# Feed-forward of a decoder layer: banks, the addition of z, and two folded constants

## The chip, the cores and the metric

The kernel runs on one core of a Trainium2 chip. The metric is device time in microseconds of one execution, from the chip. Before the change the median of three runs is 3090.13 us (3086.34 to 3092.24). A core has engines that work side by side, each with its own queue of instructions: TensorE (PE in the profile, with its weight loads as PEld), VectorE (DVE), ScalarE (ACT), GpSimd (POOL) and SyncE (SP), which here issues DMAs. SBUF is the working memory of 128 partitions; PSUM has eight banks, each holding 128x512 fp32 values, and matmuls write there.

## What is computed

One decoder layer in fp32 over 2048 tokens of width 512: self-attention over a gathered cache, cross-attention, and a feed-forward part with a low-rank correction; each is added to its input and then normalised. The feed-forward part, where the change lies:

```python
z = jnp.einsum('bsd,od->bso', x, W) + b
u = jnp.einsum('bsd,edr->ebsr', x, A)
m = jnp.einsum('ebsr,ero,e->bso', u, B, p_scores)
norm_z = jnp.linalg.norm(z, axis=-1, keepdims=True)
norm_m = jnp.linalg.norm(m, axis=-1, keepdims=True)
gamma = jnp.minimum(C_CLAMP * norm_z / (norm_m + EPS), 1.0)
return z + gamma * m
...
x = _layernorm(x + ffn(x))
```

C_CLAMP is 0.5, EPS is 1e-6, the small term of the layer norm is 1e-5.

## The kernel before

Tokens stand in four blocks of 512 (tb = 0 to 3), each of four row tiles of 128 tokens (i = 0 to 3). `acc[tb]` holds the running sum with tokens on partitions, `xT[tb]` the same with features on partitions. Self-attention comes first (to about 1900 us), then keys and values of the cross-attention, then 32 cross-attention units (8 groups of heads by 4 blocks), and last the feed-forward part of each block.

The loop over units (variable n) is software-pipelined: in step n stand the queries and scores of unit n and the attention (`attend`) and output projection (`project`, seven matmul steps on three PSUM banks x, y, z) of unit n−1. When the last group of a block is projected, the block is normalised (`layernorm_parts`, lines L149 to L157) and a step later transposed (`transpose_block`, L129 and L131; two of its four copies are VectorE's and two ScalarE's). The feed-forward calls lie at the end: block 0 at the end of step 31; then, in the closing step 32, the transposes of block 2, `attend(31)`, the feed-forward of block 1, the projection of unit 31; after it blocks 2, then the transposes of block 3, then block 3.

TensorE and GpSimd work in program order from step 31 on: their order is written out by hand. VectorE's and ScalarE's orders are chosen there by a scheduler when the program is built; on the chip every engine then takes its queue strictly in order.

`feed_forward(tb)` per block: pu (L1172, the low-rank u, four chunks of features, two matmuls each), uT (L1176, VectorE scales pu out of PSUM). Then for each row tile: pz (L1186, four chunks) and pm (L1185, one chunk, needs uT), pm standing between the second and third chunk of pz; sqm (L1191) and sqz (L1195), ScalarE's squares summed into `nrm`; z = pz + bias by VectorE (L1193); acc + z by GpSimd (L1196); nrm's root by ScalarE (L1197); four small VectorE instructions that make gam (L1199 to L1202); acc += gam times pm (L1203, VectorE); the layer norm of the tile: statistics (L167, L169), rstd = variance + small term (L171, VectorE), its root (L172, ScalarE), its reciprocal (L173, VectorE), the scaling of acc (L174, VectorE); and the store (L1206).

PSUM's eight banks in this part: four of tag ps, handed out in turn (queries, projections, transposes, pu, pz, pm); two of tag sc (scores of a unit); po0 and po1 (`pp`, the first half of `attend`'s result, `pox`). `bank` gives a tile of tag ps.

Of the kernel before, what the change touches and what calls it, by code (L numbers as in the profile page):

```python
# [9 lines left out]
F32 = mybir.dt.float32  # L10
I32 = mybir.dt.int32
AF = mybir.ActivationFunctionType
ALU = mybir.AluOpType
# [3 lines left out]
P = 128  # L17
DIM = 512
# [4 lines left out]
TB = 512  # L23
NTB = NT // TB
TPB = TB // P
NC = DIM // P
# [19 lines left out]
LN_EPS = 1e-5  # L46
NORM_EPS = 1e-6
CLAMP = 0.5
# [4 lines left out]
def decoder_layer(  # L53
# [30 lines left out]
    nc = tc.nc  # L84

    const = ctx.enter_context(tc.tile_pool(name="const", bufs=1))
# [5 lines left out]

    ident = const.tile([P, P], F32, name="ident")
    make_identity(nc, ident)
    bk = const.tile([P, NKV], F32, name="bk")
    bv = const.tile([P, NKV], F32, name="bv")

# [21 lines left out]
    def bank(shape, name, tag=None):  # L119
        if tag in special:  # L120
            v = special[tag]
            return v.rearrange("p (a b) -> p a b", a=shape[1])
        return psum[-1].tile(shape, F32, tag=tag or "ps", name=name)
# [17 lines left out]
    def layernorm_parts(tb, name):  # L141
        a = acc[tb]
        rstd = small.tile([P, TPB], F32, tag="rstd", name=f"rstd_{name}_{tb}")
        mv = small.tile([P, TPB, 2], F32, tag="mv", name=f"mv_{name}_{tb}")

        def stats():
            for j in range(TPB):
                st = small.tile([P, 6], F32, tag="st", name=f"st_{name}_{tb}_{j}")
                nc.vector.bn_stats(st, a[:, j, :])  # L149
                nc.vector.bn_aggr(mv[:, j, :], st)  # L150
            nc.vector.tensor_scalar_add(rstd, mv[:, :, 1], LN_EPS)
            nc.scalar.activation(rstd, rstd, AF.Sqrt)

        def scale():
            nc.vector.reciprocal(rstd, rstd)
            for j in range(TPB):
                nc.vector.tensor_scalar(  # L157
                    a[:, j, :], a[:, j, :], mv[:, j, 0:1], rstd[:, j : j + 1],
                    ALU.subtract, ALU.mult,
                )  # L160

        return stats, scale

    def layernorm_tile(tb, j, name):
        a = acc[tb][:, j, :]
        st = small.tile([P, 6], F32, tag="st", name=f"st_{name}_{tb}_{j}")
        nc.vector.bn_stats(st, a)  # L167
        mv = small.tile([P, 2], F32, tag="mv1", name=f"mv_{name}_{tb}_{j}")
        nc.vector.bn_aggr(mv, st)  # L169
        rstd = small.tile([P, 1], F32, tag="rstd1", name=f"rstd_{name}_{tb}_{j}")  # L170
        nc.vector.tensor_scalar_add(rstd, mv[:, 1:2], LN_EPS)  # L171
        nc.scalar.activation(rstd, rstd, AF.Sqrt)  # L172
        nc.vector.reciprocal(rstd, rstd)  # L173
        nc.vector.tensor_scalar(a, a, mv[:, 0:1], rstd, ALU.subtract, ALU.mult)  # L174

# [288 lines left out]
    with ExitStack() as ph:  # L464
# [3 lines left out]
        sc = ph.enter_context(tc.tile_pool(name="sc", bufs=2, space=PSUM))  # L468
# [309 lines left out]
        c = first.c  # L778
        first.step(1)
        first.step(2)  # L780
        z = first.mul("z", 5, True)
# [156 lines left out]
    with ExitStack() as ph:  # L938
# [23 lines left out]
        with ExitStack() as st:  # L962
# [16 lines left out]
            for k, (gp, tb) in enumerate(pairs):  # L979
                if gp == 1:  # L980
                    stats, scale = layernorm_parts(tb, "a")
# [29 lines left out]
        sc = ph.enter_context(tc.tile_pool(name="xsc", bufs=2, space=PSUM))  # L1011
        pp = ph.enter_context(tc.tile_pool(name="xpo", bufs=1, space=PSUM))
# [154 lines left out]

        def feed_forward(tb):
            wf, af, bm = ffn_w
            pu = bank([P, TB], f"pu{tb}")  # L1170
            for c in range(NC):
                nc.tensor.matmul(  # L1172
                    pu, af[:, c, :], xT[tb][:, c, :], start=(c == 0), stop=(c == NC - 1)
                )
            uT = sb.tile([P, TB], F32, tag="uT", name=f"uT{tb}")
            nc.vector.tensor_scalar(uT, pu, pe, None, ALU.mult)  # L1176
            for i in range(TPB):
                u = f"{tb}_{i}"
                cols = slice(i * P, (i + 1) * P)
                a = acc[tb][:, i, :]  # L1180
                pz = bank([P, DIM], f"pz{u}")
                pm = bank([P, DIM], f"pm{u}")
                for c in range(NC):
                    if c == 2:
                        nc.tensor.matmul(pm, uT[:, cols], bm, start=True, stop=True)  # L1185
                    nc.tensor.matmul(  # L1186
                        pz, xT[tb][:, c, cols], wf[:, c, :], start=(c == 0), stop=(c == NC - 1)
                    )
                nrm = small.tile([P, 2], F32, tag="nrm", name=f"nrm{u}")
                sqm = sb.tile([P, DIM], F32, tag="en", name=f"sqm{u}", bufs=3)  # L1190
                nc.scalar.activation(sqm, pm, AF.Square, accum_out=nrm[:, 1:2])  # L1191
                z = sb.tile([P, DIM], F32, tag="en", name=f"z{u}", bufs=3)
                nc.vector.tensor_tensor(z, pz, bz, ALU.add)  # L1193
                sqz = sb.tile([P, DIM], F32, tag="en", name=f"sqz{u}", bufs=3)
                nc.scalar.activation(sqz, z, AF.Square, accum_out=nrm[:, 0:1])  # L1195
                nc.gpsimd.tensor_tensor(a, a, z, ALU.add)  # L1196
                nc.scalar.activation(nrm, nrm, AF.Sqrt)  # L1197
                gam = small.tile([P, 1], F32, tag="gam", name=f"gam{u}")
                nc.vector.tensor_scalar_add(gam, nrm[:, 1:2], NORM_EPS)  # L1199
                nc.vector.reciprocal(gam, gam)  # L1200
                nc.vector.tensor_tensor(gam, gam, nrm[:, 0:1], ALU.mult)
                nc.vector.tensor_scalar(gam, gam, CLAMP, 1.0, ALU.mult, ALU.min)  # L1202
                nc.vector.scalar_tensor_tensor(a, pm, gam, a, ALU.mult, ALU.add)  # L1203
                layernorm_tile(tb, i, "f")
                r0 = tb * TB + i * P
                nc.sync.dma_start(out=out[r0 : r0 + P, :], in_=a)  # L1206
# [42 lines left out]
        for n in range(N + 1):  # L1249
# [6 lines left out]
            if n < N:  # L1256
                g, tb = units[n]
# [28 lines left out]
            if n == N:  # L1286
                feed_forward(1)
# [6 lines left out]
            if n < N and g == 0:  # L1294
                for j in range(TPB):
                    a = acc[tb][:, j, :]
# [20 lines left out]
            if n == N - 1:  # L1317
                feed_forward(0)
        scales.pop(0)()
        feed_forward(2)  # L1320
        while later:
            later.pop(0)()
# [50 lines left out]
```

## Time and profile before

| | |
|---|---|
| median of three runs | 3090.13 us |
| the profiled execution's own time | 3088.83 us |
| its span, first to last instruction | 3085.9 us |
| busy: TensorE / VectorE / ScalarE / GpSimd | 3034.2 / 2186.5 / 757.2 / 967.6 us |
| granted TensorE clock, mean over the span | 0.997 |

Where the last 120 us go, by windows of the trace (us in the window, then busy us of each engine with the number of instructions, the granted clock, the DMA share and GB/s):

```profile
2960.00:2980.00 20.00, 20.00 (x67) 12.35 (x66) 15.90 (x37) 4.16 (x10) 1.27 (x1) 1.00 0.12 26
2980.00:3000.00 20.00, 18.35 (x65) 8.83 (x63) 18.54 (x44) 7.43 (x23) 6.04 (x5) 1.00 0.11 41
3000.00:3020.00 20.00, 19.96 (x57) 10.86 (x58) 14.98 (x37) 7.10 (x23) 7.90 (x7) 1.00 0.10 39
3020.00:3040.00 20.00, 19.02 (x63) 11.41 (x62) 14.68 (x38) 2.36 (x8) 1.27 (x1) 1.00 0.07 27
3040.00:3060.00 20.00, 17.10 (x52) 8.25 (x51) 17.71 (x42) 6.22 (x21) 3.81 (x3) 1.00 0.14 53
```

The columns are PE, PEld, DVE, ACT and POOL. A busy TensorE means that a matmul was in its pipeline. In a timeline row stand the start in us from the span's start, the length, the engine, the line, the operation, what it writes and reads, and in brackets how long the engine had been idle before it and what ended that.

### The profile page before, as it was taken

What the parts mean: (1) busy time and instruction counts of PE and PEld (TensorE: products, weight loads), DVE (VectorE), ACT (ScalarE), POOL (GpSimd) and SP (SyncE); (2) the same over time, 40 slices, a digit from 0 to 9 for tenths busy, and PEclk for the clock granted to TensorE, in tenths of its full rate; (3) what the DMA queues carried; (4) which work ended last, traced back from release to release, by engine and by line L of the source; (5) the groups of instructions that cost most, each with busy time, mean ns of one, the idle gap of its engine ahead of it and who ended that gap; (6) DMA issues with size and microseconds to landing.
All of it is one profiled execution on the core that took longest, in us unless ns stands there. A gap on an engine that the chain in (4) does not pass through costs nothing.

```text
span 3085.9 us, 42306 instructions
## 1 busy us (share of the span) xinstructions
PE 3034.2 (98%) x14944; PEld 2320.6 (75%) x14944; DVE 2186.5 (71%) x3957; ACT 757.2 (25%) x1760; POOL 967.6 (31%) x789
## 2 busy tenths in 40 slices
PE   8999999999999999999999999999999999999998
PEld 6777677777777777777777769988888888888764
DVE  6777877877877877877877764436656666666677
ACT  2323232232332232232232221211111111111122
POOL 4221322321321322322322123136444444454421
PEclk9999999999999999999999999999999999999999
DMA  6444444444444444444344343321121121121101
GB/s 210 115 115 119 113 115 122 111 122 114 109 126 115 103 129 113 106 126 115 100 125 112 96 122 138 110 96 52 52 69 49 49 69 49 49 68 49 48 28 41
DMA packets 200913, 298.66 MB, mean 97 GB/s; under 512 B 44160, under 2 KB 94848, under 8 KB 200704
## 3 DMA queue, kind: packets, MB, share of 16 engines
q1 hardware_dynamic: 187328, 282.51, 33.8%
q10 hardware_dynamic: 11328, 9.26, 1.0%
q0 software_dynamic: 2048, 4.20, 0.5%
q8 instruction: 120, 1.97, 0.3%
q14 instruction: 89, 0.73, 0.1%
HBM read 107.05 MB, written 20.97 MB: 41 GB/s over the span
## 4 chain that ended last, share of the span: by engine, by line
PE 91%; DVE 4%; DMA 2%; SPq 2%; ACT 1%; issue 1%; ACTq 0%; DVEq 0%
PE po L661 15%; PE s L615 15%; PE sx L1043 2%; PE pox L1114 2%; PE w_0y L282 1%; PE q_3y L282 1%; PE wx_2y L282 1%; PE wx_1y L282 1%; PE w_3y L282 1%; SPq L653 1%; PE qx_2y L282 1%; PE qx_3y L282 1%; PE qx_0y L282 1%; PE w_1y L282 1%; PE q_2y L282 1%; PE wx_0y L282 1%
## 5 line engine op out<-in xcount | busy, mean ns | idle before, releaser
L623 ACT ACTIVATE p<-s,nmax 128x576 f32<-128x576 f32 x512 | 380.4, 743 | 1207.7 <-DVE nmax L620 1207.6
L615 PE MATMUL s<-kT,qT 128*128 128x288 f32 x2048 | 577.9, 408 | 10.4 <-ACT p L623 9.7
L661 PE MATMUL po<-pT,v 128*128 128x512 f32 (+1 forms) x1280 | 549.2, 602 | 4.1 <-DMA pT<-T 4.1
L615 PEld LDWEIGHTS s<-kT,qT 128*128 128x128 f32 x2048 | 387.5, 190 | 115.0 <-issue 20.1
L620 DVE TENSOR_REDUCE nmax<-s 128x1 f32<-128x576 f32 x512 | 384.4, 751 | 47.6 <-PE s L615 47.1
L641 DVE STREAM_TRANSPOSE T<-p 128x576 f32<-128x576 f32 x512 | 394.5, 770 | 4.4
L661 PEld LDWEIGHTS po<-pT,v 128*128 128x128 f32 (+1 forms) x1280 | 213.7, 189 | 204.1 <-issue 177.0
L633 DVE TENSOR_SCALAR p<-p,den 128x576 f32<-128x576 f32 x512 | 324.2, 633 | 17.9
L632 DVE RECIPROCAL den<-den 128x1 f32<-128x1 f32 x512 | 84.1, 164 | 238.1 <-ACT p L623 238.1
L256 POOL TENSOR_TENSOR so<-oT,oT 128x512 f32<-128x512 f32 x32 | 42.5, 1327 | 648.5 <-ACT oT L684 648.5
L258 POOL TENSOR_TENSOR so<-oT 128x512 f32<-128x512 f32 x32 | 40.7, 1271 | 334.4 <-PE w_1y L282 93.0
L1222 POOL TENSOR_TENSOR txx<-x1T 128x512 f32<-128x512 f32 x31 | 39.5, 1275 | 229.5 <-PE qx_3z L282 93.1
L197 POOL TENSOR_TENSOR tx<-xT 128x512 f32<-128x512 f32 x31 | 39.7, 1280 | 206.6 <-PE q_3z L282 65.4
L623 ACT ACTIVATION_READ_ACCUMULATOR p<-s,nmax 128x1 f32 x512 | 99.7, 195 | 0.0
L256 POOL TENSOR_TENSOR sox<-oTx,oTx 128x512 f32<-128x512 f32 x32 | 40.5, 1267 | 184.1 <-DVE oTx L1134 178.6
L1060 ACT ACTIVATE ex<-ex 128x512 f32<-128x512 f32 x64 | 39.4, 632 | 203.2 <-DVE ex L1059 203.2
L684 ACT COPY oT<-po 128x512 f32<-128x512 f32 x128 | 72.0, 588 | 44.6 <-PE po L661 44.0
L1043 PEld LDWEIGHTS sx<-kvx,qTx 128*64 128x64 f32 x2048 | 62.3, 138 | 10.6 <-issue 10.6
L1132 ACT ACTIVATE oTx<-pox,bv 128x256 f32<-128x256 f32 x128 | 52.1, 472 | 67.6 <-PE pox L1114 67.6
L1043 PE MATMUL sx<-kvx,qTx 128*64 128x64 f32 x2048 | 66.7, 224 | 0.0
L1114 PE MATMUL pox<-pTx,kvx 64*128 64x256 f32 x512 | 64.9, 390 | 1.1 <-DMA pTx<-Tx 1.1
L1134 DVE TENSOR_SCALAR oTx<-pox,bv 128x256 f32<-128x256 f32 x128 | 53.6, 479 | 11.2 <-PE pox L1114 11.2
(445 smaller groups left out, 5778.5 us busy)
## 6 DMA issues: line engine op xcount, KB each, us to landing
pT<-T SPq DMA_DIRECT2D x1020, 80.0 KB, 2.1
pT<-T SPq DMA_DIRECT2D x1016, 64.0 KB, 2.0
xT<-in_xT SPq DMA_DIRECT2D x31, 1024.0 KB, 5.6
kvx<-kv SPq DMA_DIRECT2D x32, 512.0 KB, 3.2
pTx<-Tx SPq DMA_DIRECT2D x256, 64.0 KB, 2.0
kv<-c SPq DMA_DIRECT2D x30, 512.0 KB, 3.3
wo<-in_woT SPq DMA_DIRECT2D x32, 256.0 KB, 2.9
xwq<-in_xwq SPq DMA_DIRECT2D x32, 256.0 KB, 2.6
```

What stands on the lines that cost most here:

```text
L256: nc.gpsimd.tensor_tensor(t[1], a[1, 0], a[1, 1], ALU.add)
L282: nc.tensor.matmul(self.banks[b][:, m, :], self.left[i][:, k, m * P : (m + 1) * P], self.right[i][:, k, :], start=(first and m + k == 0), ...
L615: nc.tensor.matmul(s[:, a, :HALF], qTs[n // REP][:, units[n][2], i * P : (i + 1) * P], kTs[g][:, a * HALF : (a + 1) * HALF], start=True, s ...
L620: nc.vector.tensor_reduce(nmax, s[:, :, :HALF], AX.XY, ALU.max, negate=True)
L623: nc.scalar.activation(p.rearrange("q (a k) -> q a k", a=2), s[:, :, :HALF], AF.Exp, bias=nmax, accum_out=den,)
L632: nc.vector.reciprocal(den, den)
L633: nc.vector.tensor_scalar(p, p, den, None, ALU.mult)
L641: nc.vector.transpose(Ts[n][:, :, i, :], ps_.pop((n, i)).rearrange("q (b k) -> q b k", k=SQ))
L661: nc.tensor.matmul(pos[n].rearrange("d (a q) -> d a q", a=NQD), vs[units[n][0]][rows, v, :], pTs[n // 2][rows, :, chunk, :], skip_group_ch ...
L684: nc.scalar.copy(o[:, i, :].rearrange("d (t a k) -> d a t k", t=TPB, a=NQD), pos.pop(n - 1 + i).rearrange("d (a t k) -> d a t k", a=NQD, t ...
L1043: nc.tensor.matmul(s[b * SEQ : (b + 1) * SEQ, i * REP + h, :], qTs[n][:, h, pr * HF + c0 : pr * HF + c0 + SEQ], kvs[n][:, pr, 0, c0 : c0 + ...
L1114: nc.tensor.matmul(po[pr, b][:, i, :].rearrange("d (h a j) -> d h a j", h=REP, a=2), kvs[n][r, pr, 1, i * HD : (i + 1) * HD], pTs[n][r, :, ...
```

## The change

Four edits, all but the first constant in the feed-forward part:

- A constant tile eps holds the layer norm's small term; ScalarE's root in `layernorm_tile` takes it as its bias, and VectorE's separate addition (L171) is gone. `layernorm_parts`, used for the other norms, is as it was.
- pu takes a bank of tag sc, pm takes po0 or po1 by turns; pz alone is left with the four ps banks. In the first tile of a block pm stands behind all four chunks of pz, in the other three as before.
- acc + z is made by VectorE in place of GpSimd.
- The clamp's 0.5 goes into the square of z as its scale (so `nrm` holds half of z's norm), and the last two of the four small gam instructions become one.

```diff
+    eps = const.tile([P, 1], F32, name="eps")
+    nc.gpsimd.memset(eps, LN_EPS)
...
-        nc.vector.tensor_scalar_add(rstd, mv[:, 1:2], LN_EPS)
-        nc.scalar.activation(rstd, rstd, AF.Sqrt)
+        nc.scalar.activation(rstd, mv[:, 1:2], AF.Sqrt, bias=eps)
...
-            pu = bank([P, TB], f"pu{tb}")
+            pu = sc.tile([P, TB], F32, tag="sc", name=f"pu{tb}")
...
-                pm = bank([P, DIM], f"pm{u}")
+                pm = pp.tile([P, DIM], F32, tag=f"po{i % 2}", name=f"pm{u}")
                 for c in range(NC):
-                    if c == 2:
-                        nc.tensor.matmul(pm, uT[:, cols], bm, start=True, stop=True)
                     nc.tensor.matmul(
                         pz, xT[tb][:, c, cols], wf[:, c, :], start=(c == 0), stop=(c == NC - 1)
                     )
+                    if c == (NC - 1 if i == 0 else 1):
+                        nc.tensor.matmul(pm, uT[:, cols], bm, start=True, stop=True)
...
-                nc.scalar.activation(sqz, z, AF.Square, accum_out=nrm[:, 0:1])
-                nc.gpsimd.tensor_tensor(a, a, z, ALU.add)
+                nc.scalar.activation(sqz, z, AF.Square, scale=CLAMP, accum_out=nrm[:, 0:1])
+                nc.vector.tensor_tensor(a, a, z, ALU.add)
...
-                nc.vector.tensor_tensor(gam, gam, nrm[:, 0:1], ALU.mult)
-                nc.vector.tensor_scalar(gam, gam, CLAMP, 1.0, ALU.mult, ALU.min)
+                nc.vector.tensor_scalar(gam, gam, nrm[:, 0:1], 1.0, ALU.mult, ALU.min)
```

In the program as built after the change the instructions of all engines stand as before up to pu of block 0, eps's memset aside. From there VectorE's queue has, per tile, the reciprocal of tile i directly behind its statistics and ahead of z of tile i+1, then the scaling of acc of tile i, then the addition of z of tile i+1. VectorE's four copies out of pox of unit 31, which stood among the small instructions of block 0's last tile, stand behind that tile. GpSimd's queue ends with the sums of unit 31's attention.

## The prediction

> **What bounds the kernel now.** I read the page first (shares of busy time), then the chain of waits, then the timeline of the last 120 us, where all edits but one lie.
>
> ```profile
> PE 3034.2 (98%) x14944; PEld 2320.6 (75%) x14944; DVE 2186.5 (71%) x3957; ACT 757.2 (25%) x1760; POOL 967.6 (31%) x789
> ...
> PE 91%; DVE 4%; DMA 2%; SPq 2%; ACT 1%; issue 1%; ACTq 0%; DVEq 0%
> ```
>
> TensorE is busy 98% of the span and carries 91% of the chain, so nothing in the attention stages can win or lose from this change: there all engines keep their instructions and their order. The changed part starts at 2967.85 us with pu of block 0 and ends with the kernel at 3085.9. In those 118 us the chain of waits runs mostly through VectorE. One row tile of block 2, from the timeline (start, length, engine, instruction, idle before):
>
> ```profile
> 3046.38 0.68 DVE L1193 TENSOR_TENSOR z<-pz,bz 128x512 f32<-128x512 f32 x1
> ...
> 3046.98 0.15 DVE L173 RECIPROCAL rstd_f<-rstd_f 128x1 f32<-128x1 f32 x1
> 3047.14 1.27 POOL L1196 TENSOR_TENSOR acc<-acc,z 128x512 f32<-128x512 f32 x1 [3.59 <-DVE rstd_f L173]
> 3047.16 0.63 ACT L1195 ACTIVATE sqz<-z 128x512 f32<-128x512 f32 x1 [0.46 <-DVE rstd_f L173]
> 3047.17 1.53 DVE L174 TENSOR_SCALAR acc<-acc,mv_f,rstd_f 128x512 f32<-128x512 f32 x1
> ...
> 3047.91 0.20 ACT L1197 ACTIVATE nrm<-nrm 128x2 f32<-128x2 f32 x1
> ...
> 3048.62 0.14 DVE L1199 TENSOR_SCALAR gam<-nrm 128x1 f32<-128x1 f32 x1
> ...
> 3057.24 0.15 DVE L171 TENSOR_SCALAR rstd_f<-mv_f 128x1 f32<-128x1 f32 x1
> 3057.43 0.20 ACT L172 ACTIVATE rstd_f<-rstd_f 128x1 f32<-128x1 f32 x1 [4.06 <-DVE rstd_f L171]
> ...
> 3057.66 0.16 DVE L173 RECIPROCAL rstd_f<-rstd_f 128x1 f32<-128x1 f32 x1 [0.27 <-ACT rstd_f L172]
> 3057.86 0.55 DVE L174 TENSOR_SCALAR acc<-acc,mv_f,rstd_f 128x512 f32<-128x512 f32 x1
> ```
>
> See that L174 lasts 1.53 us when GpSimd's addition starts just ahead of it and 0.55 when GpSimd is idle. From one L174 to the next (3042.31 to 3047.17) a tile takes 4.86 us on VectorE; TensorE needs ten matmul slots of 0.43 us, 4.29. So VectorE sets the pace by 0.57 us a tile.
>
> TensorE between blocks 0 and 1:
>
> ```profile
> 2990.96 1.09 PE L129 MATMUL x<-ident,acc 128*128 128x128 f32 x8 [1.08 <-DVE z L1193]
> 2991.98 2.35 PE L1114 MATMUL pox<-pTx,kvx 64*128 64x256 f32 x16
> 2994.26 3.70 PE L1172 MATMUL pu<-x1T,af 128*128 128x512 f32 x8
> 2997.79 1.88 PE L1186 MATMUL pz<-wf,x1T 128*128 128x512 f32 x4
> 3000.04 1.10 PE L1185 MATMUL pm<-bm,uT 128*128 128x512 f32 x2 [0.37 <-DVE uT L1176]
> ```
>
> The last unit's attention (pox) runs here without waiting for the block's norms, and pm of block 1 is what waits, for uT.
>
> **What the Trainium skill says.** "SBUF — State Buffer", Who interferes with whom: VectorE's two-port forms, tensor_scalar among them, and GpSimd share a port pair that one holds for its whole instruction while the other is blocked. The trace agrees (1.53 against 0.55). "VectorE: DVE Perf Modes", What auto-detection actually checks: tensor_tensor gets no doubled rate for fp32. The trace agrees: `ex<-ex,denx`, also fp32 in SBUF, 686 ns for 512 elements. "TensorE: Matmul & The Clock Gate", What's actually happening: an idle window of about 3.4 us halves the clock. After 4.05 us of idling at 2907.07 the granted clock is 0.50 here; after 2.06 us (1821.23) eight matmuls took their usual time.
>
> **The change part by part**, on the profiled execution's clock. "gam(b,i)" is the start of the first gam instruction (L1199) of tile i of block b.
>
> *VectorE adds z; small terms.* Per tile, start to start. Before: L174 1.44, gam chain to L1203 0.83, L1203 0.78, statistics 0.73 and 0.22, L171 0.07, z 0.60, reciprocal 0.19: 4.86. After, in the changed order (reciprocal, then z, L174, the addition, gam): the three gam instructions left 0.64 (one of 0.19 gone); L1203 0.78; statistics 0.73; aggregate to reciprocal 0.46, since L171 no longer stands between and VectorE waits for ScalarE's root (0.18 + 0.04 + the 0.24 seen at 3057.43 to 3057.66); reciprocal 0.19; then z to gam. On VectorE that is 0.60 + 0.48 (L174 without GpSimd; four L157 take 1.91) + 0.60 to 0.67 for the addition, taken from the 0.69 of the nearest rows, 1.68 to 1.75; through ScalarE it is what it was, z start to gam 1.78 (3062.91 to 3064.69). The later one counts, 1.77. Sum 4.57 to 4.58, so 0.29 less a tile, not the 0.98 that L174 loses: the addition takes most of it back. Bounds: 4.29 (TensorE's pace, if VectorE is faster than I think) to 4.86 (the 0.27 wait for the root is longer, all gained lost). TensorE's 4.29 stays below.
>
> *pm behind all of pz in a block's first tile.* sqm now starts after pz, and ScalarE does sqm (0.70), sqz (0.75), nrm (0.24) in a row: gam at pm's end + 1.73. In block 0 pm ends at 75.74 (times from here on less 2900), so gam at 77.5, as before (77.50, from a z at 75.78); the addition is hidden in this wait. Where pm waited for uT, the wait is covered by two more pz chunks.
>
> *Banks, block 0 to 1.* gam(0,0) 77.50, three tiles to 91.24. Two copies x1T (0.60 each) fall between the addition and the last gam, as before: L1203 of tile 3 starts at 93.09 and ends 93.84 (before 95.23). But its pm now lies in bank po1, and pox's second matmul writes po1. It waits there, with everything behind it on TensorE's hand-written order: the rest of pox, pu(1), pz(1,0). TensorE is there at 91.2 and idles about 2.7 us. Then pox 1.75, pu 3.44, pz 3.44, pm with its end 1.02, ScalarE 1.73: gam(1,0) at 105.3, before 104.67. So 0.6 is lost where 1.4 was ahead: this wait costs 2.0.
>
> *Block 1 and the last projection.* Three tiles: 0.87 less, gam(1,3) 0.24 early. TensorE ends the block at 116.3, does three projection steps (5.19) to 121.46 and the second x step; before, that step started at 121.27, held by L353. It is now held by TensorE itself, 0.2 later, without the 0.26 wait shown inside it, so the projection ends where it did. Balance 0.
>
> *Block 2.* pu ends at 131.9, pz follows without waiting for uT (134.15), pm ends 136.32, gam(2,0) 138.05 against 138.88: 0.83 ahead. Tiles 0.87: 1.70. *Block 3.* pu starts after the x1T copies, 1.7 ahead; pu to gam is 9.63 for 9.78: 0.15. Tiles 0.87. Tail gam to L174: 2.82 for 3.17: 0.35. **Sum: 1.70 + 0.15 + 0.87 + 0.35 = 3.1 us.**
>
> *Hidden or nil.* The memset of eps (0.1 us) falls into GpSimd's 1.50 us wait before its first gather at 3.40. Square's scale and the root's bias change operands, not lengths (bounds: 0 to 0.02 each, 16 tiles, off the sum). pu in bank sc frees a bank nobody was late for. eps moves later tiles in SBUF by a few bytes; no row of the trace shows a length that hangs on a tile's place (pT<-T and pTx<-Tx, 64 KB each, both land in 2.0 us).
>
> Own execution: 3088.83 − 3.1 = 3085.7. It lies 1.3 below the median of 3090.13; in proportion the forecast is **3087.0**. About 0.2%, 6.2 us, is what a measurement of this kernel can tell from no change, and 3.1 is half of that.
>
> **Rivals.**
> *A, the clock halves* in the 2.7 us idling before pox: priced by 2907.07, where 8 matmuls took 3.54 and 2.80 for 1.73: 2.9 us. All later blocks move: 3089.9. Against: 2.7 is short of the 4.05 that did it.
> *B, faster:* TensorE becomes the bound (4.29 a tile) and the wait at po1 is not felt. From the forecast: block 0's 0.87 and the 2.0, of which block 1 keeps all as TensorE carries it; blocks 2 and 3 another 0.87 each: 3.1 + 0.87 + 2.0 + 1.74 = 7.7, time 3082.4. For: TensorE's 4.29 is near. Against: the po1 wait is in the order, and ScalarE's 1.77 doesn't shrink. A part of it plus the spread of the runs shown (3086.34 to 3092.24) can also carry a true 4 beyond 6.2.
> *C, slower:* VectorE's reciprocal now waits on ScalarE's queue, where sqm of the next tile (0.60 + 0.20) stands ahead of the root, and z, L174, the addition all stand behind that reciprocal. If sqm comes late, 0.80 is added in each of the 12 tiles that have a next one: +9.6 − 3.1, time 3096.6. It decides from the point where pm of tile i+1 ends later than 0.74 before the aggregate of tile i ends. Against: block 0's first tile has pm at 78.3, the aggregate at 79.84, 0.8 us to spare, and more in later ones.
> *D, the change doesn't do it:* L174 stays at 1.5 without GpSimd. Then the addition comes on top, about 0.7 a tile, 3098. The 0.55 above speaks against it.
>
> **Numbers.** Forecast 0.62, A 0.10, B 0.20, C 0.06, D 0.02. A and the forecast are within 0.2%: 0.72; faster 0.20; slower 0.08. Range: the forecast's own bounds 3084 to 3090, widened by the spread of runs and towards B: 3082 to 3092.
>
> **What would show it.** L174 near 0.55 in all 16; no GpSimd addition after the last sums; a tile every 4.6 us; a wait of 2 to 3 us of TensorE for L1203 before pox; the reciprocal idle about 0.3 after the aggregate. Wrong if tiles stay at 4.86 or fall to 4.3, if the clock drops after that wait, or if the first 2967 us change.

## The result and the profile after

| | before | after |
|---|---|---|
| median, 22 runs each | 3089.06 us (3086.34 to 3092.24) | 3085.07 us (3082.36 to 3088.27) |
| ratio, 95% interval | | 0.9987 (0.9981 to 0.9992) |
| the profiled execution, its span | 3088.83, 3085.9 us | 3084.9, 3083.0 us |

The kernel is 0.13% faster, 4.0 us by the medians and 2.9 us by the spans of the two profiled executions. The interval lies below 1, but the gain is within the 0.2% named in the prediction. Two lines of the page of the kernel after, busy time by engine and the shares of the chain that ended last, and one of its costliest groups (busy time in us, mean ns of one, then idle time ahead of it and how much of that its main releaser ended):

```profile
PE 3035.2 (98%) x14944; PEld 2321.5 (75%) x14944; DVE 2181.4 (71%) x3941; ACT 756.6 (25%) x1760; POOL 947.6 (31%) x774
...
PE 92%; DVE 3%; SPq 1%; ACT 1%; DMA 1%; issue 1%; ACTq 0%; DVEq 0%
...
L1115 PE MATMUL pox<-pTx,kvx 64*128 64x256 f32 x512 | 66.3, 395 | 2.1 <-DVE acc L1205 2.1
```

GpSimd lost 20 us of work and VectorE 5; TensorE has the same 14944 matmuls. The last line shows that in all 512 matmuls of pox TensorE idles 2.1 us, all of it for L1205 (L1203 of the kernel before).

The rest is read from the stretch that the change touches, from the start of pu of block 0 to the end of the last VectorE instruction. Before it lasts 115.16 us, after 112.48: 2.68 of the span's 2.9 lie there. All 16 scalings of acc, in the view of one line's instructions (shortest, median and longest in ns):

```profile
L175 DVE TENSOR_SCALAR acc<-acc,mv_f,rstd_f x16: 536/538/547, 2980.4 to 3079.5; 128x512 f32<-128x512 f32 x16
```

Before, 13 of the 16 took 1.52 to 1.61 us (the 1.61 stood beside GpSimd's sums of unit 31, the other twelve beside its additions). One row tile of block 2 after the change, from the timeline:

```profile
3045.40 0.18 DVE L171 BATCH_NORM_AGGREGATE mv_f<-st_f 128x2 f32<-128x6 f32 x1
...
3045.61 0.29 ACT L173 ACTIVATE rstd_f<-mv_f,eps 128x1 f32<-128x1 f32 x1 [0.85 <-DVE mv_f L171]
3045.94 0.16 DVE L174 RECIPROCAL rstd_f<-rstd_f 128x1 f32<-128x1 f32 x1 [0.36 <-ACT rstd_f L173]
3046.02 0.67 DVE L1196 TENSOR_TENSOR z<-pz,bz 128x512 f32<-128x512 f32 x1
...
3046.61 0.54 DVE L175 TENSOR_SCALAR acc<-acc,mv_f,rstd_f 128x512 f32<-128x512 f32 x1
3046.73 0.63 ACT L1198 ACTIVATE sqz<-z 128x512 f32<-128x512 f32 x1 [0.82 <-DVE z L1196]
...
3047.06 0.69 DVE L1199 TENSOR_TENSOR acc<-acc,z 128x512 f32<-128x512 f32 x1
...
3047.48 0.20 ACT L1200 ACTIVATE nrm<-nrm 128x2 f32<-128x2 f32 x1
3047.72 0.15 DVE L1202 TENSOR_SCALAR gam<-nrm 128x1 f32<-128x1 f32 x1
```

A tile takes 4.47 us (before 4.87, both from one gam to the next). The reciprocal now stands ahead of z on VectorE, which idles 0.36 us there for ScalarE's root; before, z stood there and covered the root.

TensorE between blocks 0 and 1, from the timeline:

```profile
2988.18 1.99 PE L131 MATMUL x<-ident,acc 128*128 128x128 f32 x16
2990.10 0.70 PE L1115 MATMUL pox<-pTx,kvx 64*128 64x256 f32 x2
2992.93 3.36 PE L1115 MATMUL pox<-pTx,kvx 64*128 64x256 f32 x14 [2.14 <-DVE acc L1205]
2996.22 3.97 PE L1175 MATMUL pu<-x1T,af 128*128 128x512 f32 x8
3000.03 3.60 PE L1187 MATMUL pz<-wf,x1T 128*128 128x512 f32 x8
```

The wait at po1 is there, and 14 matmuls of pox, which took 1.99 us at full clock in r5 below, take 3.36. The same place by windows of the trace (length, then busy time and instructions of PE, PEld, DVE, ACT, POOL, then the granted clock, DMA share, GB/s):

```profile
2986.56:2989.97 3.41, 3.41 (x21) 2.27 (x19) 2.94 (x8) 2.05 (x5) 0.00 (x0) 1.00 0.14 51
2989.97:2993.39 3.42, 1.28 (x8) 0.73 (x8) 3.31 (x8) 0.82 (x4) 0.00 (x0) 1.00 0.21 77
2993.39:2996.80 3.41, 3.41 (x15) 2.28 (x12) 2.36 (x8) 1.86 (x5) 0.00 (x0) 0.50 0.21 77
2996.80:3000.21 3.41, 3.41 (x9) 1.51 (x8) 0.41 (x2) 0.00 (x0) 2.75 (x3) 1.00 0.00 0
```

The clock is halved for 3.41 us, just when TensorE resumes. So rival A of the prediction happened. TensorE is busy through all of it, and at half the clock that costs half of it, 1.7 us. Compared directly, pox's resume to gam of block 1's first tile takes 13.16 us here and 11.52 in r5 below, which kept the clock: 1.64.

### The profile page after: what moved, and what is told of

Read it like the earlier page. It is cut to its first block, busy times and chain, and to the rows that moved or that the text cites. A ratio compares the mean times of both kernels' runs of the same rounds, so it can differ in the third digit from the quotient of the medians.

```text
span 3083.0 us, 42247 instructions
## 1 busy us (share of the span) xinstructions
PE 3035.2 (98%) x14944; PEld 2321.5 (75%) x14944; DVE 2181.4 (71%) x3941; ACT 756.6 (25%) x1760; POOL 947.6 (31%) x774
## 4 chain that ended last, share of the span: by engine, by line
PE 92%; DVE 3%; SPq 1%; ACT 1%; DMA 1%; issue 1%; ACTq 0%; DVEq 0%
PE po L662 15%; PE s L616 15%; PE sx L1044 2%; PE pox L1115 2%; PE w_0y L283 1%; PE wx_1y L283 1%; PE q_3y L283 1%; PE wx_2y L283 1%; PE w_3y L283 1%; PE wx_3y L283 1%; SPq L654 1%; PE qx_2y L283 1%; PE qx_3y L283 1%; PE qx_0y L283 1%; PE w_1y L283 1%; PE wx_0y L283 1%
## 5 line engine op out<-in xcount | busy, mean ns | idle before, releaser
L1115 PEld LDWEIGHTS pox<-pTx,kvx 64*128 64x128 f32 x512 | 48.3, 189 | 17.5 <-issue 10.1
```

The source lines that it names most:

```text
L1115: nc.tensor.matmul(po[pr, b][:, i, :].rearrange("d (h a j) -> d h a j", h=REP, a=2), kvs[n][r, pr, 1, i * HD : (i + 1) * HD], pTs[n][r, :, ...
```

## The experiments

Because the halved clock fell into some executions and not into others, the table gives the stretch as traced and, as an estimate, at full clock: less half of the time in which TensorE was busy at the halved clock. "Tile" is from one gam to the next, "time" one execution, except where the number of runs is given. Single times don't rank the runs: pu of block 0, ahead of which all do the same work, starts anywhere from 2966.5 to 2970.9 us.

| run | stretch | at full clock | tile | time |
|---|---|---|---|---|
| before | 115.16 | 115.2 | 4.87 | 3088.83 |
| after | 112.48 | 110.8 | 4.47 | 3084.9 |
| r1, after again | 112.46 | 110.8 | 4.47 | 3083.86 |
| r2, after without the po1 wait | 108.01 | 108.0 | 4.47 | 3079.69 |
| r3, after without the banks | 109.79 | 109.8 | 4.47 | 3082.54 |
| r4, r12, z by VectorE alone | 109.04, 109.03 | 109.0 | 4.35 | 3081.66 (r12, 13 runs) |
| r5, after with GpSimd adding z | 110.84 | 110.8 | 4.60 | 3084.37 |
| r6, the banks alone | 120.07 | 116.0 | 4.86 | 3092.47 |
| r7, after without eps | 113.43 | 111.7 | 4.57 | 3089.59 |
| r9, the folded constants alone | 112.25 | 110.5 | 4.60 | 3086.03 |
| r10, z and the gam fold | 112.49 | 110.8 | 4.57 | 3086.20 |
| r8, r11, r2 with z ahead | 107.48, 107.47 | 107.5 | 4.29 | 3081.21 (r11, 8 runs) |

**r1: the kernel after, once more.** No edit.

> The changed kernel once more. The measure for all these runs is the feed-forward stretch in the trace: from the start of pu(0) to the end of the last VectorE instruction, 115.16 us before (2967.85 to 3083.01) and 112.48 after (2967.58 to 3080.06). If the halved TensorE clock behind the wait for bank po1 belongs to the kernel: a stretch of 112.5, granted clock 0.5 in the 2 us behind that wait. If it was an accident of the one profiled execution: full clock there and a stretch near 110.6.

Stretch 112.46, and the clock halved again, from 2992.12 to 2995.53. The tiles repeat to 0.01 us. What the repeat alone couldn't tell is taken up in the last section: by the estimate there the halving isn't bound to happen in every execution.

**r2: pm of block 0 in a bank of tag sc.** Nothing of block 0 is then in po1 when pox comes.

```diff
-                pm = pp.tile([P, DIM], F32, tag=f"po{i % 2}", name=f"pm{u}")
+                pm = (pp if tb else sc).tile(
+                    [P, DIM], F32, tag=f"po{i % 2}" if tb else "sc", name=f"pm{u}"
+                )
```

> The changed kernel, but block 0's pm lies in the two sc banks, so pox (the last unit's attention) finds po0 and po1 free. Theory (the wait for po1 costs 2 us and more, and the halved clock behind it 2 more): pox follows the transposes at once, full clock, gam(1,0) 4.5 us earlier, and all of it is kept to the end: stretch 108.0. Rival (TensorE runs ahead of VectorE there anyway and the last projection gives it back): 111.5 to 112.5.

The stretch is 108.01. TensorE runs through, from its timeline:

```profile
2987.58 2.00 PE L131 MATMUL x<-ident,acc 128*128 128x128 f32 x16
2989.51 2.00 PE L1115 MATMUL pox<-pTx,kvx 64*128 64x256 f32 x16
2991.43 3.70 PE L1175 MATMUL pu<-x1T,af 128*128 128x512 f32 x8
```

Block 1's first gam comes 4.46 us earlier than in the kernel after, and the end 4.47 earlier: nothing behind absorbs it. Of that 1.64 is the clock and 2.83 the wait.

**r3: without the banks.** pu and pm from `bank` again, pm behind two chunks of pz in every tile; all else as after.

```diff
-            pu = sc.tile([P, TB], F32, tag="sc", name=f"pu{tb}")
+            pu = bank([P, TB], f"pu{tb}")
...
-                pm = pp.tile([P, DIM], F32, tag=f"po{i % 2}", name=f"pm{u}")
+                pm = bank([P, DIM], f"pm{u}")
```

> The changed kernel with the banks undone: pu and pm in ps again, pm before the third chunk of pz in every tile. Theory (VectorE's tile of 4.47 us makes the gain; the banks cost more by the po1 wait and the clock than the covered uT waits give): 110.2. Rival (the banks and pm's place make the gain, because TensorE no longer waits for uT): 115 or more.

109.79. Against r2 the banks are worth 1.78 us as long as they bring no wait: in r3 the transposes before pox wait 0.45 us for a ps bank that z still holds, and pm of block 2 waits 0.63 for uT; r2 has neither wait. With the wait at po1 they cost 1.05 at full clock, and 2.69 as the kernel after was traced.

**r4: z by VectorE alone.** One line of the kernel before is changed.

```diff
-                nc.gpsimd.tensor_tensor(a, a, z, ALU.add)
+                nc.vector.tensor_tensor(a, a, z, ALU.add)
```

> The kernel before with one part of the change: z is added by VectorE. Here VectorE still takes z of the next tile ahead of the reciprocal, so the root on ScalarE is hidden. Theory: a tile is 4.86 - 0.96 (L174 without GpSimd) + 0.62 (the addition) = 4.5, no wait for po1: stretch 111 to 112. Rival (the addition takes back all that L174 loses): a tile of 4.86, stretch 115.2.

109.04, better than expected. A tile takes 4.35 where the whole change has 4.47, and its timeline shows the difference:

```profile
3042.52 0.15 DVE L171 TENSOR_SCALAR rstd_f<-mv_f 128x1 f32<-128x1 f32 x1
3042.59 0.68 DVE L1193 TENSOR_TENSOR z<-pz,bz 128x512 f32<-128x512 f32 x1
3042.71 0.20 ACT L172 ACTIVATE rstd_f<-rstd_f 128x1 f32<-128x1 f32 x1 [1.21 <-DVE rstd_f L171]
...
3043.19 0.15 DVE L173 RECIPROCAL rstd_f<-rstd_f 128x1 f32<-128x1 f32 x1
...
3043.31 0.69 DVE L1196 TENSOR_TENSOR acc<-acc,z 128x512 f32<-128x512 f32 x1
...
3043.92 0.54 DVE L174 TENSOR_SCALAR acc<-acc,mv_f,rstd_f 128x512 f32<-128x512 f32 x1
```

z still stands ahead of the reciprocal and covers ScalarE's root: no bracket, no idling. The scheduler turned the two round in every run here that has the gam edit and was left to it (after, r1, r2, r3, r5, r7, r9, r10), and in no other (before, r4, r6, r12).

**r5: after, but GpSimd adds z.**

```diff
-                nc.vector.tensor_tensor(a, a, z, ALU.add)
+                nc.gpsimd.tensor_tensor(a, a, z, ALU.add)
```

> The changed kernel with the addition of z back on GpSimd, all else as changed. In this VectorE queue the scaling of acc stands directly behind z of the next tile, so it is issued about 0.6 us after z starts, while GpSimd can start only when z has ended (0.76). Theory of the prediction (GpSimd's addition blocks the scaling, 1.53 us): a tile of about 4.9, stretch 115.5 to 116. Rival (who issues first holds the port: here VectorE does, so the scaling takes 0.55 and GpSimd waits): a tile of 4.5 to 4.65, stretch 112.5 to 114, and then it was the order, not the engine of the addition, that took the block away.

The scalings take 0.54 although GpSimd adds. From the timeline:

```profile
3046.17 0.54 DVE L175 TENSOR_SCALAR acc<-acc,mv_f,rstd_f 128x512 f32<-128x512 f32 x1
...
3046.34 1.51 POOL L1199 TENSOR_TENSOR acc<-acc,z 128x512 f32<-128x512 f32 x1 [3.10 <-DVE z L1196]
```

VectorE's scaling starts first and keeps its length; GpSimd's addition takes 1.51 in place of 1.27. So the new order alone takes the blocked 1.53 away, whichever engine adds. That fits what the Trainium skill says under "SBUF — State Buffer", Who interferes with whom: the one that issues first keeps the shared ports. Moving the addition then brings the tile from 4.60 to 4.47. Over the stretch that gains nothing: r5's 110.84 (its clock stayed up, and it is below both of its forecasts) stands against 110.8 at full clock with the addition on VectorE. What the tiles gain is lost between the blocks. From block 2's last gam to block 3's first r5 takes 9.80 us and the kernel after 10.45, because there the addition stands ahead of VectorE's copies x1T, behind which pu of block 3 starts.

**r6: the banks alone**, on the kernel before, with pm behind all of pz in a block's first tile.

```diff
-            pu = bank([P, TB], f"pu{tb}")
+            pu = sc.tile([P, TB], F32, tag="sc", name=f"pu{tb}")
...
-                pm = bank([P, DIM], f"pm{u}")
+                pm = pp.tile([P, DIM], F32, tag=f"po{i % 2}", name=f"pm{u}")
...
-                    if c == 2:
-                        nc.tensor.matmul(pm, uT[:, cols], bm, start=True, stop=True)
...
+                    if c == (NC - 1 if i == 0 else 1):
+                        nc.tensor.matmul(pm, uT[:, cols], bm, start=True, stop=True)
```

> The kernel before with the banks alone: pu in sc, pm in po0 and po1, pm behind pz in a block's first tile. Theory (the po1 wait and the clock cost about 4 us, the covered uT waits give less): tiles of 4.86, stretch 116.7, slower than before by 1.5. Rival (the banks are what gains): 113.

120.07, slower than before. TensorE's wait for po1 and its clock, from the timeline and from windows:

```profile
2995.05 3.78 PE L1114 MATMUL pox<-pTx,kvx 64*128 64x256 f32 x14 [3.04 <-DVE acc L1203]
```

```profile
2989.70:2993.11 3.41, 1.35 (x7) 0.71 (x6) 3.33 (x7) 1.96 (x6) 1.26 (x1) 1.00 0.00 0
2993.11:2996.52 3.41, 1.47 (x8) 1.21 (x10) 2.70 (x9) 0.20 (x1) 0.00 (x0) 0.50 0.21 77
2996.52:2999.94 3.42, 3.42 (x12) 1.98 (x9) 2.26 (x6) 1.57 (x5) 0.03 (x1) 0.50 0.16 59
```

The clock is halved for 6.83 us here and for 3.41 more in block 3 (2.45 and 1.6 us lost). So 120.07 misses the expected 116.7, which had a loss by the clock in it, by 3.4. At full clock it is 116.0: 0.9 worse than before, near the 1.05 that r3 gives.

**r7: after, with the small term added by VectorE again.**

```diff
-        nc.scalar.activation(rstd, mv[:, 1:2], AF.Sqrt, bias=eps)
+        nc.vector.tensor_scalar_add(rstd, mv[:, 1:2], LN_EPS)
+        nc.scalar.activation(rstd, rstd, AF.Sqrt)
```

> The changed kernel without eps: VectorE adds the small term again, then ScalarE's root, then the reciprocal, all ahead of z of the next tile as in the changed order. Theory: aggregate to reciprocal 0.65 for 0.54, a tile 4.58, stretch 113.6. Rival (the root with a bias tile, 0.29 for 0.20, costs as much as the addition it saves): 112.5.

Tile 4.57, stretch 113.43 with one halved period as in the kernel after. In the new order, where the small term, the root and the reciprocal all lie in VectorE's way, eps saves 0.10 a tile and 0.95 us in all.

**r9 and r10: what turns the order.** r9 is the kernel before with eps in the root, the clamp's half in the square and three gam instructions; GpSimd adds z, the banks are as before. r10 is r4 with the square's scale and the gam edit alone. The diff is r9's; r10 has its second part:

```diff
-        nc.vector.tensor_scalar_add(rstd, mv[:, 1:2], LN_EPS)
-        nc.scalar.activation(rstd, rstd, AF.Sqrt)
+        nc.scalar.activation(rstd, mv[:, 1:2], AF.Sqrt, bias=eps)
...
-                nc.scalar.activation(sqz, z, AF.Square, accum_out=nrm[:, 0:1])
+                nc.scalar.activation(sqz, z, AF.Square, scale=CLAMP, accum_out=nrm[:, 0:1])
...
-                nc.vector.tensor_tensor(gam, gam, nrm[:, 0:1], ALU.mult)
-                nc.vector.tensor_scalar(gam, gam, CLAMP, 1.0, ALU.mult, ALU.min)
+                nc.vector.tensor_scalar(gam, gam, nrm[:, 0:1], 1.0, ALU.mult, ALU.min)
```

> The kernel before with the folded constants alone (eps in the root, 0.5 in the square, one gam instruction less); z is added by GpSimd, all banks as before. Built so, VectorE's queue has the reciprocal ahead of z and the scaling of acc directly behind z. Theory from the run with the addition back on GpSimd (whoever issues first holds the port, and here that is the scaling): the scaling takes 0.55 in all tiles, a tile 4.6, stretch 111. Rival (the fold saves its one instruction, 0.19 a tile, and GpSimd still blocks the scaling): a tile of 4.7, the scaling 1.53, stretch 113 or more.

> The kernel before with z added by VectorE and the gam fold, no eps, no banks. The fold takes one of four small instructions away, but the queue built with it has the reciprocal directly behind the small term's addition, with z of the next tile behind it. Theory (the exposed root costs more than the fold saves): a tile of 4.57 against 4.35 with z alone, stretch 110.8 to 111.2 against 109.04. Rival (an instruction less is a gain): 4.2 to 4.3, stretch 108 to 108.5.

Both have the order of the kernel after. r9's tile, from the timeline:

```profile
3045.03 0.16 DVE L174 RECIPROCAL rstd_f<-rstd_f 128x1 f32<-128x1 f32 x1 [0.36 <-ACT rstd_f L173]
3045.11 0.67 DVE L1194 TENSOR_TENSOR z<-pz,bz 128x512 f32<-128x512 f32 x1
3045.70 0.53 DVE L175 TENSOR_SCALAR acc<-acc,mv_f,rstd_f 128x512 f32<-128x512 f32 x1
3045.86 1.50 POOL L1197 TENSOR_TENSOR acc<-acc,z 128x512 f32<-128x512 f32 x1 [3.10 <-DVE z L1194]
```

The constants alone, without moving the addition, unblock the scaling by turning the order: 15 of r9's 16 scalings take 0.53 to 0.55 (the other, beside GpSimd's sums of unit 31, 1.61). r10 shows that the gam edit is enough to turn it; eps alone wasn't run. The traced stretches, 112.25 and 112.49, hold one period of halved clock each, not at po1 but at pu of block 3, from windows of r9:

```profile
3049.11:3052.52 3.41, 1.70 (x14) 1.26 (x13) 2.88 (x8) 2.11 (x6) 1.51 (x1) 1.00 0.21 77
3052.52:3055.93 3.41, 3.41 (x5) 1.33 (x6) 2.55 (x6) 0.29 (x1) 0.00 (x0) 0.50 0.00 0
```

At full clock they are 110.5 and 110.8, near the 111 and 110.8 to 111.2 expected. Adding the gam edit to r4 thus costs 1.8 us at full clock: it saves one instruction of about 0.19 a tile, and with the order it brings the reciprocal's wait into every tile.

**r8, r11 and r12: versions that gain more.** r8 and r11 are the same kernel: r2, and VectorE's order in the tile loop written by hand. Pz, pm, sqm and z of tile i+1 (`front`) stand between the root and the reciprocal of tile i:

```diff
+                    nc.scalar.activation(rstd, mv[:, 1:2], AF.Sqrt, bias=eps)
+                    if i + 1 < TPB:
+                        made = front(i + 1)
+                    nc.vector.reciprocal(rstd, rstd)
```

r12 is r4, timed in several rounds.

> The changed kernel with block 0's pm in the sc banks and VectorE's order in the feed-forward written by hand: z of the next tile stands between the aggregate and the reciprocal, so ScalarE's root is hidden. Theory (the wait for the root costs 0.36 a tile and TensorE's 4.29 is the next bound): tiles of 4.3, stretch 106.5 to 107.5. Rival (the path through ScalarE, z to square to root to gam, sets the tile whatever the order): tiles of 4.47, stretch as with block 0's pm in sc alone, 108.0.

> The version of r8 timed: all parts of the change, block 0's pm in the sc banks, z ahead of the reciprocal by hand. Its stretch was 107.48 for 115.16 before. If nothing outside the stretch changes: 7.7 us less than before, ratio 0.9975. If the parts outside shift by more: anything between 0.996 and 0.999.

> The version of r4 timed: one line of the change alone, z added by VectorE. Stretch 109.04 for 115.16: 6.1 us less, ratio 0.9980, so better than the whole change (0.9987) and behind r11.

From the timeline of r11:

```profile
3037.84 0.69 DVE L1198 TENSOR_TENSOR z<-pz,bz 128x512 f32<-128x512 f32 x1 [0.40 <-PE pz L1189]
...
3042.06 0.30 ACT L1222 ACTIVATE rstd_f<-mv_f,eps 128x1 f32<-128x1 f32 x1 [0.96 <-DVE mv_f L1220]
3042.13 0.69 DVE L1198 TENSOR_TENSOR z<-pz,bz 128x512 f32<-128x512 f32 x1
3042.74 0.15 DVE L1225 RECIPROCAL rstd_f<-rstd_f 128x1 f32<-128x1 f32 x1
```

z covers the root again, and a tile takes 4.29 us (4.59 behind a block's first): TensorE's ten matmul slots of 0.43 now set the pace. The first row, from behind a block's first tile, shows VectorE waiting for pz. Stretch 107.47, median 3081.21 us against 3088.52 of the kernel before on the same chip, ratio 0.9975 (0.9964 to 0.9985). r12, one line of the change, gives 3081.66, ratio 0.9979 (0.9971 to 0.9987). Between these two the times don't decide; by the stretch r11 is 1.56 us ahead. Both beat the kernel before beyond 0.2% in the median, though the upper ends of both intervals lie inside it.

## Why the prediction was right

It gave 3087.0 us and no measurable change as the likeliest; 3085.07 was measured, within 3082 to 3092. The mechanism held, but several terms of the sum were mis-sized, in opposite directions, and one of the prediction's own signs of being wrong came: the clock dropped after the wait. That the traced gain of 2.68 lies near the forecast 3.1 is in part luck, as the sum below shows.

**Right.** The scaling fell to 0.54 in all 16 tiles, so D is out (though r5 and r9 show that the turned order does this with GpSimd adding, too); the addition costs VectorE 0.69 and so takes most of it back; GpSimd ends with unit 31's sums; the reciprocal idles 0.36 where "about 0.3" was forecast; TensorE waits for L1203 before pox (2.14 us for a forecast of 2.7: two matmuls of pox went ahead, 0.70). C didn't come: ScalarE always began the root as soon as the aggregate was there. B didn't come in the kernel after, whose tile of 4.47 stays above 4.29; it is what r11 reaches once order and bank are changed.

**The tile, 4.58 forecast, 4.47 measured.** Three terms: reciprocal to z 0.08 in place of 0.19; z to gam 1.70 for 1.77; against these aggregate to reciprocal 0.54 for 0.46, since ScalarE's root with eps as its bias takes 0.29 and not 0.20: the prediction had put what the bias costs at 0 to 0.02. A tile gains 0.40, not 0.29; from block 2's first gam to the end the gain is 2.85 where the prediction's terms give 0.87 + 0.15 + 0.87 + 0.35 = 2.24.

**The wait at po1, priced at 2.0.** r2 shows what was ahead without it: block 1's first gam 2.77 us earlier than before, not 1.4. With the wait and at full clock it comes about when it came before, so the wait costs 2.83.

**Rival A, left at 0.10.** It took the 4.05 us gap at 2907.07 as the nearest row, called 2.7 short of it, and made the price from that gap, 2.9. What failed is reading the length of a gap as what decides: 2.14 us was enough. Nor was the prediction's other row, 2.06 us without harm, evidence against A. At the same place in r4 a gap of the same length was followed by the halved clock, and the same eight matmuls took 5.37 us for 3.67. First the kernel before, then r4:

```profile
1821.23 3.67 PE L661 MATMUL po<-pT,v 128*128 128x512 f32 x8 [2.06 <-DMA pT<-T]
```

```profile
1821.80 5.37 PE L661 MATMUL po<-pT,v 128*128 128x512 f32 x8 [2.07 <-DMA pT<-T]
```

The price was 1.64, as only one period of 3.41 us was halved; at 2907.07 in the kernel before it was two.

**"Balance 0" at the last projection.** This presupposed that TensorE arrives with 0.6 lost. It arrived 1.69 late, and the projection, which waits for nothing but TensorE, passed it on:

```profile
3022.38 1.89 PE L283 MATMUL wx_3x<-xwo,oTx 128*128 128x256 f32 x8
...
3029.28 3.17 PE L1175 MATMUL pu<-x1T,af 128*128 128x512 f32 x7
```

No bracket stands in the first of these rows, where before 0.36 of waiting for L353 stood; pu of block 2 starts 1.27 later after block 0's pu than before (61.70 for 60.43). From pu to gam the new place of pm wins 1.10 back (forecast 0.83). At block 2's first gam the kernel is 0.17 behind, where 0.83 ahead was forecast; at full clock it would be some 1.5 ahead.

Together: −0.17 + 2.85 = 2.68 as traced. At full clock 4.3, so the forecast of 3.1 was short by 1.2, and A took 1.64 back: the two errors nearly cancel, and that is the luck. Of the 22 timed executions one was traced; of the others only a rounded mean of the clock is on record (0.996 to 0.998), which counts halved periods outside the stretch as well. So whether the medians' 4.0 is a mix of executions with and without the halved clock stays open.

## What to carry to other kernels

Removing one small instruction can turn a scheduler's order and so decide more than the instruction's own length: ask of every order what now stands between a wait and the work that used to cover it. A PSUM bank shared with a stage that comes between two uses is a wait on that stage's path; follow who writes the bank next in program order before counting banks as free. Test the parts of a bundle alone: here one line of four edits gave 6.1 us of the stretch, and the others on top of it took back 1.8 at full clock and 3.4 as traced. The parts don't add up: the constants alone give 4.6 at full clock, and the line that gives 6.1 alone gives nothing on top of the other three (r5), since the turned order has by then taken the blocked scaling away.

## What the runs showed of the hardware

**The halved clock comes in steps of 3.41 us on a grid of its own.** In every trace all changes of the clock lie a multiple of 3.413 us apart: in the kernel after it falls at 2908.05 and again at 2993.39, 25 steps later; in r6 at 2993.11 and 3057.97, 19 steps. The grid stands differently in each execution. The Trainium skill, "TensorE: Matmul & The Clock Gate", What's actually happening, says this of the window (free-running, 3413 ns), and the traces agree. But such a window needn't be idle throughout. Laying each execution's grid over the stretch gives 21 windows at full clock with less than 2.4 us of recorded matmul time. All six with at most 1.36 us were followed by a halved one, none of the ten with 1.78 or more; of the five from 1.59 to 1.71 one was (r9's, 1.70). r6's window of 1.47 us, at half clock, kept the clock down. Counted in the same way from 60 us on, the 14 traces have 21 windows with at most 1.36 us, all followed by a halved one, eight from 1.59 to 1.71, of which one was, and 115 from 1.78 to 2.4, of which again one was (r8's at 2081.09, 1.85). So the position of a gap counts as much as its length. The gaps of 2.06 and 2.07 us at 1821 show it: in the kernel before the gap lay across two windows,

```profile
1817.08:1820.49 3.41, 2.09 (x10) 1.44 (x8) 3.06 (x7) 1.87 (x4) 1.17 (x1) 1.00 0.46 113
1820.49:1823.91 3.42, 2.68 (x7) 1.27 (x8) 0.38 (x1) 0.00 (x0) 0.12 (x1) 1.00 0.34 82
```

and the clock stayed up; in r4 it lay in one, and the clock fell:

```profile
1819.24:1822.66 3.42, 1.35 (x5) 0.57 (x4) 2.04 (x4) 0.52 (x2) 1.28 (x1) 1.00 0.32 77
1822.66:1826.07 3.41, 3.41 (x5) 1.35 (x4) 0.00 (x0) 0.00 (x0) 0.00 (x0) 0.50 0.41 100
```

r5's gap of 1.73 us left one window with 1.79 us of matmul time, and the clock stayed up. From these bounds (1.6 to 1.9 us of idling in one window) a gap of 2.14 us halves the clock in an estimated half to two thirds of the positions; it did so in all three traces that have it (after, r1, r7). What exactly is counted as activity, these runs don't settle.

**Who issues first decides who is blocked.** The same two instructions took 1.53 and 1.27 us with GpSimd starting 0.03 us ahead, and 0.54 and 1.51 with VectorE 0.17 us ahead.

**ScalarE's root of 128 values took 0.29 us with eps as its bias (after) and 0.20 without (r7).** Its input changed as well, a column of mv in place of rstd, and no run separates the two. VectorE saves an instruction of 0.15, the root grows by 0.09, and eps is worth 0.10 a tile.
